# Layer 3 in tiles of two, plain last LSTM units, a new start and norms on ScalarE in a four-layer graph network

## The chip, the cores and the metric

The kernel runs on one core of one Trainium2 chip. The metric is the device time of one execution in microseconds (us). Before the change it is 2455.06 us, the median of three runs (2454.82, 2455.06, 2457.53). A core has five engines[...]: TensorE (PE; its weight loads are the row PEld) for matrix products, VectorE (DVE), ScalarE (ACT), GpSimd (POOL) and SyncE (SP), which here only starts transfers (DMAs). ScalarE can start transfers too. Products land in PSUM, everything else lies in SBUF.

## The reference

The input x has 128 graphs of 64 nodes with 256 features, and one 64x64 adjacency matrix `adj`. Four layers follow, each with a residual sum and a layer norm:

```python
x = _layernorm(x + L0(x, adj))   # A_hat x, two linear layers, each with a batch norm over all rows
x = _layernorm(x + L1(x, adj))   # Chebyshev-like aggregation by 2L/lambda_max - I, attention, GELU MLP
x = _layernorm(x + L2(x, adj))   # two GCN layers, then LSTMs over windows of 1, 2, 3 and 4 nodes
x = _layernorm(x + L3(x, adj))   # graph attention
```

What bears on the change:

- Layer 0: `deg = sum of A+I over rows + sum over columns - diagonal`, `dinv = deg**-0.5`, `A_hat = (A+I) * dinv * dinv`.
- Layer 1 needs the largest eigenvalue of the adjacency matrix.
- Layer 2: for p = 1 to 4 the nodes are cut into windows of p; an LSTM runs over the p nodes of a window and its last state replaces the last node of the window. Each p works on what the one before left.
- Layer 3: `Wh = h W`, `e[i,j] = s1[i] + s2[j]` with `s1 = Wh a1`, `s2 = Wh a2`; a leaky ReLU (slope 0.2), minus infinity where `adj` is 0, softmax over j, `h' = attention @ Wh`.

All arithmetic is float32.

## The kernel before, in words

**Tiling.** The 128 graphs are 16 blocks of 8. A block is four tiles of 128 rows (two graphs each) by 256 features: 128x1024 numbers. `tm` sees a slot as four tiles (rows on partitions), `fm` as two chunks of features on partitions. Four blocks form a group (`hT[g]`, tiles named h77 to h80). There are four PSUM tiles of 128x1024 (`PS`) and a stock of SBUF slots of the same size (`mem`), into which buffers of earlier layers are put back when they are no longer needed, so that a slot can be called x70, h77, rows or wL.

**Order.** Work is written as Python generators, which yield steps (engine, estimated time, PSUM tiles and slots needed) ahead of the instructions. `flow` runs streams of such generators: each stream has a width (how many at once) and a priority. At each turn it takes the step that can start soonest by its estimates, so the estimates set the order of the instructions on every engine; it is fixed when the program is built. Changing an estimate or a stream's width reorders instructions far away.

**Start (lines 236 to 427).** The adjacency matrix goes twice, block-diagonally, into `bdA` and its transpose into `bdAT`, all four on SP, and into `adj2` (two on ScalarE, for the masks `cap1` and `cap3`). Block 0 of x and W1 follow on ScalarE's queue; W2 and six small columns go on SP ahead of the other blocks of x. VectorE adds the identity, takes three sums and combines them (L410 to L421), POOL takes the power -1/2 (L422), and a TensorE product (L426) and a VectorE scaling (L427) give `AhT`, which the first aggregation (helper L324) needs.

**Layer 0.** `first_block` aggregates a block (L324), multiplies by W1 (L348) and takes statistics; `eig` finds the eigenvalue by 26 squarings meanwhile. After the first batch norm `second_block` multiplies by W2 (L554); after the second, `end_block` applies it (ScalarE, L625), transposes (L342), adds x (VectorE, L633) and ends with `ln_steps`.

**Layer norms.** `stats` (L275 to L277) takes mean and variance per tile on VectorE, POOL takes the power -1/2 of four numbers a row, about 1.03 us. Then `ln_steps` lets VectorE subtract and multiply, four instructions (L288); `ln_steps_act` lets VectorE make the product -mean*rstd (L313) and ScalarE do scale and bias, four instructions (L316). Before the change `ln_steps` ends layers 0 and 1, `ln_steps_act` serves layer 3.

**Layer 2.** A unit (`unit`, `lstm`) is an LSTM over all windows of one p in a group. Its first step is plain (L932). For the further steps the kernel uses a form of Strassen's multiplication on two halves of the windows: seven products instead of eight, in stages (`stage1` to `stage4`, helper L1000), with copies and sums on VectorE (L1059, L1066, L1068), copies on ScalarE (L1038, L1040) and differences on VectorE and POOL between them. `units_of` makes two units of p = 4 for the last group, of 16 windows times 16 graphs, so that their halves have 128 columns.

**Layer 3 (`last_block`).** One block at a time: load x (L1273), bring the state back to rows (ScalarE L1278, TensorE L342), add, norm, transpose (L336), multiply by W with two more columns for s1 and s2 (L1308), 16 small score products of 64x64 (L1327, L1330), leaky ReLU and softmax on ScalarE and VectorE (L1337 to L1350), division by the sum on POOL (L1352), transposition (L1358, L1360), aggregation (L1366), residual (L1370), norm, store (L1374). Two blocks of the first three groups may run at once, at the lowest priority, four of the last group, at a high one. Two LSTM units may run at once.

Of the kernel before, what the change touches and what calls it, by code (L numbers as in the profile page):

```python
# [15 lines left out]
P = 128  # L16
# [16 lines left out]
def kernel(ctx: ExitStack, tc: tile.TileContext, a: dict, out: bass.AP):  # L33
# [206 lines left out]
    for s in range(2):  # L240
        h = halves[s]
        nc.sync.dma_start(bdA[h, h], a["adj"])
        nc.sync.dma_start(bdAT[h, h], a["adjT"])
        nc.scalar.dma_start(adj2[h, :], a["adj"])
        for m in (bdA, bdAT):
            G.memset(m[h, halves[1 - s]], 0.0)
# [9 lines left out]

    cap1 = ctile([P, N], "cap1")
    V.tensor_scalar(cap1, adj2, 0.0, BIG, ALU.is_gt, ALU.mult)
    V.tensor_scalar(cap1, cap1, -1.0e9, None, ALU.add)

    cap3 = ctile([P, N], "cap3")
    V.tensor_scalar(cap3, adj2, 0.0, 2.0, ALU.not_equal, ALU.mult)
    V.tensor_scalar(cap3, cap3, -1.0, BIG, ALU.add, ALU.mult)

# [4 lines left out]
    def stats(y, n=NT):  # L269

        st = sm.tile([P, n, 6], F32, tag="ln_st", name="ln_st")
# [33 lines left out]
    def ln_steps_act(y):  # L305

        yield step("V", 2.7)
        mv, rs = stats(y)
        yield step("G", 1.0)
        G.tensor_tensor(rs, rs, neghalf[:, :NT], ALU.pow)  # L310
        yield step("V", 0.2)
        nm = sm.tile([P, NT], F32, tag="ln_nm", name="ln_nm")
        V.scalar_tensor_tensor(nm, mv[:, :, 0], -1.0, rs, ALU.mult, ALU.mult)  # L313
        yield step("S", 2.4)
        for t in range(NT):
# [16 lines left out]
    def to_fm(ps, y):  # L332

        for c in range(2):
            for t in range(NT):
                T.transpose(ps[:, c, t * P : (t + 1) * P], y[:, t, c * P : (c + 1) * P], ident)  # L336

    def to_tm(ps, yT):

        for t in range(NT):  # L340
# [48 lines left out]
    with c0:  # L389
        ep = c0.enter_context(tc.tile_pool(name="eig", bufs=2))  # L390

        first = mem.take()
        nc.scalar.dma_start(tm(mem[first]), x_blk[0])
        W1T = load_w(wp, "W1T", a["L0_gnn_W1"], queue=nc.scalar)
        W2T = load_w(wp, "W2T", a["L0_gnn_W2"])
        cols = {k: load_col(wp, f"l0{k}", a[f"L0_gnn_{k}"]) for k in ("b1", "g1", "be1", "b2", "g2", "be2")}
# [11 lines left out]

        An = ctile([P, P], "An", wp)
        V.tensor_tensor(An, bdA, ident, ALU.add)  # L410
        tmp = etile("etmp")
        V.tensor_tensor(tmp, bdAT, ident, ALU.add)
        d3 = etile("d3", 3, 1)
        V.reduce_sum(d3[:, 0:1], An, axis=AX.X)
        V.reduce_sum(d3[:, 1:2], tmp, axis=AX.X)
        tmp = etile("etmp")
        V.tensor_tensor(tmp, An, ident, ALU.mult)
        V.reduce_sum(d3[:, 2:3], tmp, axis=AX.X)
        dinv = etile("dinv", 1, 1)
        V.tensor_tensor(dinv, d3[:, 0:1], d3[:, 1:2], ALU.add)  # L420
        V.tensor_tensor(dinv, dinv, d3[:, 2:3], ALU.subtract)  # L421
# [10 lines left out]
        def eig():  # L432
            Sy = etile("Sy", bufs=1)
            yield step("V", 1.2)
            V.tensor_tensor(Sy, bdA, bdAT, ALU.add)
# [75 lines left out]
        def first_block(i):  # L511
            if i:
# [3 lines left out]
            else:  # L516
                xs = first
# [53 lines left out]
        tasks = [(None, lambda: first_block(0), 1), (None, eig, 0)]  # L571
        tasks += [(None, lambda i=i: first_block(i), 2) for i in blocks if i]
# [45 lines left out]
    def end_block(i):  # L618
# [17 lines left out]
        yield from ln_steps(x)  # L636
        mark("end", i)

    def block(i):
# [196 lines left out]
        yield from ln_steps(x)  # L836
# [13 lines left out]
    av = load_w(gw, "av", a["L3_gnn_a"])  # L850
    bl = load_col(gw, "bih", a["L2_gnn_bih"])
# [50 lines left out]
    def lstm(p, n, parts, x_of, out_of):  # L902
# [79 lines left out]
        mem.give(s_o)  # L982

# [138 lines left out]

    def gcn_block(i):
# [61 lines left out]
    def unit(p, g, w0, nw, b0, nb):  # L1185
# [4 lines left out]
        parts = [(slice(q * hn, (q + 1) * hn), nw // 2 if even else nw) for q in range(2)]  # L1190

        def half(ap, q):

            if even:
# [74 lines left out]
    def last_block(i):  # L1269
        yield step("Q", 4.0, sl=1)  # L1270
        s_x = mem.take()
        x = tm(mem[s_x])
        nc.sync.dma_start(x, XD[i])  # L1273
        yield step("S", 2.2, sl=1)
        s_h = mem.take()
        hb = fm(mem[s_h])
        for c in range(2):
            S.copy(hb[:, c, :].rearrange("p (b n) -> p b n", b=8), hT_block(i)[:, c, :, :].rearrange("p n b -> p b n"))  # L1278
        yield step("T", 1.0, ps=1)
        ps = PS.take()  # L1280
        to_tm(tm(PS[ps]), hb)
        mem.give(s_h)
        mark("read", i)
        yield step("V", 1.3, ps=-1)
# [245 lines left out]
```

## Time and profile before

| | us or share |
|---|---|
| the profiled execution | 2454.4 |
| its span, first to last instruction | 2452.6 |
| TensorE busy | 2353.9 (96%) |
| VectorE / ScalarE / POOL busy | 1274.4 / 1095.9 / 572.8 |
| mean granted TensorE clock | 0.982 |
| last LSTM products run | 2376.2 to 2376.9 |
| last store issued at | 2448.73 |

The busy time of TensorE includes stretches at a lower clock, in which the same product takes longer. Share of busy time is an average over stages with different limits, so the tables by stretches of time say more: each line gives a stretch, its length, the busy time of each engine in it (with the number of instructions), the granted clock, the busy share of the DMA engines and the GB/s moved. In the answers on single instructions the first number is the start, the second the duration, both in us, and brackets hold the idle time before and what ended it. A product of float32 with 128 or 256 columns stands as two records in the trace, a transposition as one.

### The profile page before, as it was taken

How to read it: one execution, taken by the hardware profiler on the slowest of the kernel's cores; microseconds unless marked ns; L12 is line 12 of the kernel's file. 1: busy time of each engine (PE TensorE's matmuls, PEld its weight loads, DVE VectorE, ACT ScalarE, POOL GpSimd, SP SyncE). 2: the span in 40 equal slices, each digit the busy share in tenths (PEclk: the TensorE clock that was granted, in tenths of full speed). 3: DMA queues.
4: the chain of work that ended last, by engine and by line, in shares of the span. 5: the costliest groups of instructions: out<-in, count | busy, mean ns of one | idle time of the engine just before them, and what ended most of it. 6: DMA issues, size and time to landing. Idle time of an engine off the chain costs nothing. (4 is left out here: it accounts for less than half of the span.)

```text
span 2452.6 us, 35349 instructions
## 1 busy us (share of the span) xinstructions
PE 2353.9 (96%) x14468; PEld 1818.8 (74%) x14468; DVE 1274.4 (52%) x2965; ACT 1095.9 (45%) x1916; POOL 572.8 (23%) x416
## 2 busy tenths in 40 slices
PE   8999888999999999999999999999999999999986
PEld 5544466767667767675766888899999889888874
DVE  4542387657455645484552433345344455455664
ACT  2256332333444343434434444445435465556774
POOL 0000034233323222343132222222222221222211
PEclk9999899999999999999999999999999999999997
DMA  5110110100000000000100000000000010000111
GB/s 171 43 52 0 40 36 27 44 3 15 1 9 10 18 9 10 1 9 35 44 26 11 16 1 1 1 18 1 1 1 18 1 35 10 26 18 18 61 53 44
DMA packets 40499, 57.60 MB, mean 23 GB/s; under 512 B 4624, under 2 KB 33936, under 8 KB 40336
## 3 DMA queue, kind: packets, MB, share of 16 engines
q1 hardware_dynamic: 39376, 54.25, 6.8%
q8 instruction: 113, 1.85, 0.3%
q10 hardware_dynamic: 960, 1.08, 0.1%
q14 instruction: 50, 0.41, 0.1%
HBM read 38.55 MB, written 16.78 MB: 23 GB/s over the span
## 5 line engine op out<-in xcount | busy, mean ns | idle before, releaser
L1000 PE MATMUL ps<-x,x 128*128 128x256 f32 (+1 forms) x1024 | 228.4, 360 | 0.0
L1000 PEld LDWEIGHTS ps<-x,x 128*128 128x128 f32 x1024 | 179.8, 190 | 19.5 <-DVE t L1046 0.4
L1000 PE MATMUL ps<-t,x 128*128 128x256 f32 (+1 forms) x800 | 178.5, 359 | 1.4 <-ACT x L1040 1.4
L1000 PEld LDWEIGHTS ps<-t,x 128*128 128x128 f32 x800 | 140.5, 190 | 18.9 <-ACT x L1040 2.0
L932 PE MATMUL ps<-h,wL 128*128 128x144 f32 (+2 forms) x552 | 131.8, 393 | 0.0
L348 PE MATMUL ps<-t,W1T 128*128 128x512 f32 x256 | 116.0, 597 | 0.0
L932 PEld LDWEIGHTS ps<-h,wL 128*128 128x128 f32 x552 | 87.9, 190 | 37.7 <-issue 36.8
L285 POOL TENSOR_TENSOR ln_rs<-ln_rs,neghalf 128x4 f32<-128x4 f32 x48 | 49.6, 1033 | 202.1 <-DVE ln_rs L277 202.0
L944 ACT ACTIVATE t<-ps,bih 128x512 f32<-128x512 f32 (+3 forms) x116 | 68.5, 642 | 57.7 <-PE ps L932 57.6
L275 DVE BATCH_NORM_STATS2 ln_st<-x 128x6 f32<-128x256 f32 x240 | 92.0, 403 | 0.7
L1059 DVE COPY x<-ps 128x256 f32<-128x256 f32 (+3 forms) x84 | 30.7, 366 | 118.6 <-PE ps L1000 118.5
L297 POOL TENSOR_TENSOR ln_rs<-ln_rs,neghalf 128x4 f32<-128x4 f32 x32 | 36.6, 1145 | 230.9 <-DVE ln_rs L277 230.8
L1076 ACT ACTIVATE x<-x,bih 128x512 f32<-128x512 f32 (+3 forms) x84 | 53.1, 632 | 77.9 <-DVE x L1066 77.7
L932 PE MATMUL ps<-h,x 128*128 128x256 f32 x384 | 87.1, 379 | 0.8 <-ACT t L1152 0.8
L1000 PE MATMUL ps<-h,x 128*128 128x256 f32 (+1 forms) x416 | 84.4, 333 | 1.1 <-DVE x L1059 0.6
L932 PEld LDWEIGHTS ps<-h,x 128*128 128x128 f32 x384 | 72.7, 190 | 10.9 <-ACT t L1152 1.2
L348 PEld LDWEIGHTS ps<-t,W1T 128*128 128x128 f32 x256 | 46.2, 191 | 45.9 <-issue 45.9
L288 DVE TENSOR_SCALAR x<-x,ln_mv,ln_rs 128x256 f32<-128x256 f32 x144 | 63.3, 495 | 31.5 <-POOL ln_rs L285 31.5
L1066 DVE TENSOR_TENSOR x<-ps,x 128x512 f32<-128x512 f32 (+3 forms) x84 | 48.5, 579 | 57.4 <-PE ps L1000 46.1
L1076 ACT ACTIVATE t<-t,bih 128x512 f32<-128x512 f32 (+3 forms) x59 | 36.9, 629 | 86.1 <-DVE t L1066 85.9
L944 ACT ACTIVATE x<-ps,bih 128x512 f32<-128x512 f32 (+3 forms) x88 | 51.6, 639 | 50.2 <-PE ps L932 50.1
L276 DVE BATCH_NORM_AGGREGATE ln_mv<-ln_st 128x2 f32<-128x6 f32 x448 | 71.5, 166 | 0.0
(663 smaller groups left out, 5691.6 us busy)
## 6 DMA issues: line engine op xcount, KB each, us to landing
t<-in_x_dram SPq DMA_DIRECT2D x25, 512.0 KB, 4.0
xd<-x SPq DMA_DIRECT2D x16, 512.0 KB, 2.6
x<-xd SPq DMA_DIRECT2D x8, 512.0 KB, 3.3
out_dram<-x SPq DMA_DIRECT2D x8, 512.0 KB, 2.9
h<-in_x_dram SPq DMA_DIRECT2D x6, 512.0 KB, 4.1
t<-xd SPq DMA_DIRECT2D x6, 512.0 KB, 3.3
out_dram<-t SPq DMA_DIRECT2D x6, 512.0 KB, 2.9
wL<-in_L_gnn_Wih_dram SPq DMA_DIRECT2D x2, 1024.0 KB, 5.0
```

What stands on the lines that cost most here:

```text
L275: V.bn_stats(st[:, t, :], y[:, t, :])
L276: V.bn_aggr(mv[:, t, :], st[:, t, :])
L285: G.tensor_tensor(rs, rs, neghalf[:, :NT], ALU.pow)
L288: V.tensor_scalar(y[:, t, :], y[:, t, :], mv[:, t, 0:1], rs[:, t : t + 1], ALU.subtract, ALU.mult)
L297: G.tensor_tensor(rs, rs, neghalf[:, :NT], ALU.pow)
L348: T.matmul(ps[:, c, :], w[:, k, (off + c) * P : (off + c + 1) * P], yT[:, k, :], start=(k == 0), stop=(k == nk - 1),)
L932: T.matmul(spread(fm(PS[ps])[:, j, :n], q), WL[p][0][:, k, m], x_of(0, q)[:, k], start=(k == 0), stop=(k == 1),)
L944: S.activation(of(sl)[:, j], fm(PS[ps])[:, j, :n], AF.Tanh if g == 2 else AF.Sigmoid, bias=bias(g, c))
L1000: T.matmul(dst, WS[p][name](k, g), y[:, k], start=first and k == 0, stop=k == 1, skip_group_check=not first)
L1059: V.tensor_copy(y[:, 1, :], v[:, 0, :])
L1066: V.tensor_tensor(y[:, 0:2, :], v[:, 2:4, :], y[:, 0:2, :], ALU.add)
L1076: S.activation(of(act[g])[:, 0], of(act[g])[:, 0], f, bias=bias(g, 0))
```

## The change

Five parts, in the lines of the kernel after:

1. **Start.** The four adjacency loads go two on SP and two on ScalarE. `adj2` is no longer loaded but made from `bdA` later, with the masks. Three blocks of x are loaded early, on SP, ScalarE and SP, W1 after the second. W2 and five of the six columns are issued by a task, `later_loads`, behind the first blocks. The degree comes from two VectorE instructions with a running sum.
2. **Norms.** `ln_steps_act` takes any number of tiles and replaces `ln_steps` at the end of layers 0 and 1.
3. **Layer 3.** `last_block` takes a first tile and a number of tiles; the last group goes as eight half blocks of two tiles, the others as whole blocks. The scores come from two products (block-diagonal ones times s2 spread by the identity, and the identity times s1 broadcast). The mask is applied before the leaky ReLU, which is one VectorE instruction; the maximum goes in as the bias of four exponentials, which also give the sums; the division moves behind the aggregation, into the residual sum.
4. **Last two LSTM units.** The units of 16 graphs are no longer split in halves and go by `plain_steps`: per step four pairs of gates, each of eight products of 256 columns.
5. **Streams.** The last two units have a stream of their own, so three units can run at once; four whole blocks of layer 3 may run at once instead of two; the last group's buffers are not lent again.

The diff, cut to its core:

```diff
-        nc.sync.dma_start(bdAT[h, h], a["adjT"])
-        nc.scalar.dma_start(adj2[h, :], a["adj"])
+        nc.scalar.dma_start(bdAT[h, h], a["adjT"])
...
     def ln_steps_act(y):
-        yield step("V", 2.7)
+        n = y.shape[1]
+        yield step("V", 0.68 * n)
...
-        for t in range(NT):
+        for t in range(n):
             S.activation(
...
-        first = mem.take()
-        nc.scalar.dma_start(tm(mem[first]), x_blk[0])
-        W1T = load_w(wp, "W1T", a["L0_gnn_W1"], queue=nc.scalar)
-        W2T = load_w(wp, "W2T", a["L0_gnn_W2"])
-        cols = {k: load_col(wp, f"l0{k}", a[f"L0_gnn_{k}"]) for k in ("b1", "g1", "be1", "b2", "g2", "be2")}
+        early = [mem.take() for _ in range(3)]
+        for i, q in enumerate((nc.sync, nc.scalar, nc.sync)):
+            q.dma_start(tm(mem[early[i]]), x_blk[i])
+            if i == 1:
+                W1T = load_w(wp, "W1T", a["L0_gnn_W1"], queue=nc.scalar)
...
+        def later_loads():
+            for k in cols:
+                if k != "b1":
+                    yield step("Q", 1.0)
+                    nc.sync.dma_start(cols[k], a[f"L0_gnn_{k}"])
+            yield step("Q", 6.0)
+            nc.sync.dma_start(W2T, by_chunk(a["L0_gnn_W2"]))
+            yield step("V", 1.2)
+            V.tensor_tensor(adj2, bdA[:, :N], bdA[:, N:], ALU.add)
...
+        V.scalar_tensor_tensor(Sy, bdA, 1.0, bdAT, ALU.mult, ALU.add, accum_out=d3[:, 0:1])
+        V.scalar_tensor_tensor(tmp, bdA, 1.0, ident, ALU.mult, ALU.mult, accum_out=d3[:, 1:2])
+        V.scalar_tensor_tensor(dinv, d3[:, 0:1], 1.0, d3[:, 1:2], ALU.add, ALU.subtract)
...
-        yield from ln_steps(x)
+        yield from ln_steps_act(x)
         mark("end", i)
...
-        yield from ln_steps(x)
+        yield from ln_steps_act(x)
         mark("l1", i)
...
+        if len(parts) == 1 and p > 1:
+            yield from plain_steps(p, n, us, of, bias, x_of, lambda ap: spread(ap, 0), last_h, s_cell, s_h, h_at)
+            return
...
+    def plain_steps(p, n, us, of, bias, x_of, shaped, last_h, s_cell, s_h, h_at):
+        for s in range(1, p):
+            def products(pair):
+                for j, (g, c) in enumerate(pair):
+                    for k in range(2):
+                        T.matmul(shaped(dst), WL[p][0][:, k, m], x[:, k], start=(k == 0), stop=False)
+                    for k in range(2):
+                        T.matmul(dst, WL[p][1][:, k, m], of(s_h)[:, k], start=False, stop=(k == 1))
...
+                    S.activation(of(sl)[:, j], fm(PS[ps])[:, j, :n], AF.Tanh if g == 2 else AF.Sigmoid, bias=bias(g, c))
...
+            for c in range(2):
+                cell = of(s_cell)[:, c]
+                ta, sa = yield from products(((0, c), (2, c)))
+                tb, sb = yield from products(((1, c), (3, c)))
+                G.tensor_tensor(A[:, 1], A[:, 0], A[:, 1], ALU.mult)
+                V.tensor_tensor(cell, cell, F[:, 0], ALU.mult)
+                V.tensor_tensor(cell, cell, A[:, 1], ALU.add)
+                S.activation(A[:, 1], cell, AF.Tanh)
...
+        if nb < BG:
+            parts = [(slice(0, 2 * hn), nw)]
...
-    def last_block(i):
+    def last_block(i, t0=0, nt=NT):
...
-                T.matmul(
-                    pe[h, t, :], s12[h, t, 1:2].to_broadcast([N, N]), ident[h, h], start=True, stop=False
-                )
-        S.activation(low, pe, AF.Copy, scale=0.2)
-        V.tensor_tensor(e, pe, low, ALU.max)
-        V.tensor_tensor(e, e, bc_mid(cap3, NT), ALU.min)
-        V.tensor_tensor(e, e, bc_last(mx, N), ALU.subtract)
-        S.activation(e, e, AF.Exp)
-        V.reduce_sum(sums, e, axis=AX.X)
-        G.tensor_tensor(e, e, bc_last(sums, N), ALU.mult)
+        G.tensor_tensor(d, bc_mid(unit2, nt), bc_last(s12[:, :nt, 1], N), ALU.mult)
+        T.matmul(pe, bdones, d, start=True, stop=False)
+        T.matmul(pe, ident, bc_last(s12[:, :nt, 0], N), start=False, stop=True)
+        V.tensor_tensor(e, pe, bc_mid(cap3, nt), ALU.min)
+        V.scalar_tensor_tensor(e, e, 0.2, e, ALU.mult, ALU.max)
+            S.activation(e[:, t, :], e[:, t, :], AF.Exp, bias=mx[:, t : t + 1], accum_out=sums[:, t : t + 1])
...
-        V.tensor_tensor(x, tm(PS[ps]), x, ALU.add)
+        for t in range(nt):
+            V.scalar_tensor_tensor(
+                x[:, t, :], tm(PS[ps])[:, t, :], sums[:, t : t + 1], x[:, t, :], ALU.mult, ALU.add
+            )
...
+    last = [last_of(i) for i in range(early)]
+    end = [last_of(i, t, 2) for i in range(early, NBLK) for t in range(0, NT, 2)]
...
-            Stream(4, 2, last[early:]),
+            Stream(4, 2, end),
             Stream(2, 3, gcn),
             Stream(6, 4, seq),
-            Stream(2, 5, units),
-            Stream(2, 6, last[:early]),
+            Stream(2, 5, units[:-2]),
+            Stream(2, 5, units[-2:]),
+            Stream(4, 6, last),
```

## The prediction

> **What bounds the kernel now.** I read the page's shares and slices first, then busy time by stage, then TensorE's waits, then single instructions in time order.
>
> ```profile
> PE 2353.9 (96%) x14468; PEld 1818.8 (74%) x14468; DVE 1274.4 (52%) x2965; ACT 1095.9 (45%) x1916; POOL 572.8 (23%) x416
> ...
> PE   8999888999999999999999999999999999999986
> ```
>
> TensorE is busy for 2353.9 of 2452.6 us, so only 98.7 us of idling and the stretches at a reduced clock can be won; elsewhere an edit counts only by the TensorE work it adds or removes. The stages (columns: length, then busy PE, PEld, DVE, ACT, POOL, then PE clock, DMA share, GB/s):
>
> ```profile
> 0.00:10.00 10.00, 0.00 (x0) 0.00 (x0) 2.70 (x15) 0.11 (x1) 1.96 (x14) 1.00 0.59 168
> ...
> 290.00:300.00 10.00, 6.28 (x28) 5.91 (x29) 5.58 (x21) 5.58 (x8) 1.01 (x1) 0.50 0.32 97
> ...
> 310.00:320.00 10.00, 6.45 (x43) 5.73 (x42) 10.00 (x33) 7.61 (x11) 2.59 (x3) 0.93 0.30 100
> 320.00:330.00 10.00, 8.35 (x19) 4.40 (x20) 9.74 (x31) 1.07 (x2) 6.42 (x4) 0.56 0.00 0
> ```
>
> ```profile
> 2300.00:2377.00 77.00, 68.67 (x662) 59.15 (x660) 51.31 (x175) 56.78 (x119) 15.95 (x17) 1.00 0.19 63
> 2377.00:2453.00 76.00, 49.65 (x408) 35.62 (x408) 36.50 (x129) 39.95 (x71) 11.11 (x13) 0.77 0.11 36
> ```
>
> By such tables the 99 us lie so: 10.6 in the first 20 us, 4 at the first batch norm, 24.6 in 280-400 (entry into layer 1), 9.7 in 400-800, 7.8 in 800-2000, 7.7 in 2000-2300, 8.3 in 2300-2377, 26 after the last LSTM product (2376.9). From 310 to 390 VectorE is busy for 73 of 80 us: there it is the bound. The waits name the same places (us in total, times, longest):
>
> ```profile
> PE ps L426 <- DVE etmp L424: 10.2, 1, 10.2
> PE ps L1358 <- POOL wL L1352: 7.6, 1, 7.6
> PE ps L348 <- DVE t L782: 6.3, 1, 6.3
> ```
>
> The start and one knot at the entry into layer 1, in time order (start, duration):
>
> ```profile
> 7.07 0.29 DVE L435 TENSOR_TENSOR Sy<-bdA,bdAT 128x128 f32<-128x128 f32 x1 [2.69 <-DMA bdAT<-in_adjT_dram]
> ...
> 11.39 3.63 PE L324 MATMUL ps<-AhT,t 128*128 128x128 f32 x16 [0.45 <-DVE AhT L427]
> ...
> 299.69 0.16 DVE L894 COPY Wx<-ps 128x4 f32<-128x4 f32 x1 [3.12 <-PE ps L885]
> ```
>
> The chain of waits covers only the last 29 us: one full block going alone through scores, aggregation, norm and store.
>
> [...] block 0's 16 records from 11.39 run 0.22 us apart, later ones 0.11. [...] Here one small issue takes SP 0.57 us, but the fourth lands 3.9 us after its issue, behind block 0's load. [...] in the trace no load stands before such a norm.
>
> **The change part by part.**
>
> *Start.* Four adjacency issues sat on SP, the last from 2.62; VectorE began at 7.07. Now each queue issues two, ahead of every x block; ScalarE's two old ones (0.74 to 2.21) had landed by 3.85, so I put the start at 4.0. VectorE's chain to dinv took 2.05 us; the new one (two fused sums instead of three adds and three reductions, but with five cap instructions put between them) has about ten instructions, again 1.9. POOL, scaling, product and copy stay 2.3. Block 0's product can begin at 8.2, when its x (issued at 2.0, 4.5 to landing by the DMA table, three more 512 KB behind it) has come. Blocks 0, 1 and 2 now go in a row; the state "0 and 1 aggregated" comes at 8.2 + 3.5 (half clock) + 1.8 = 13.5 against 16.8: **-3.2 us**, between -4.5 and -1 (x or W1 late). It persists, since TensorE is 100% busy from 20 to 150. W2, columns and caps are needed only after 150.
>
> *Norms that end layers 0 and 1.* Each loses four VectorE subtract-multiplies (1.38 a block) for one 0.17 and four ScalarE activations (2.08). In ScalarE's new order nine layer-0 blocks do so before the first GELU (396 in before): VectorE -11 us, ScalarE +19, of the 110 us from 280 in which ScalarE was busy 43. Also the score-column product now precedes the first layer-1 aggregation instead of splitting it; the knot above (3.1 us of VectorE, a copy to ScalarE at 310.4 that could come at about 304) goes. Against it: ScalarE runs 15 affine activations (10.7 us) before the first norm, which so ends 3 us later than before; 16 more queue behind the second copy; and PSUM copies that feed products can stand behind a norm, 2.1 us each. TensorE idles 14.7 us in 310-390 and loses some 9 to low clock from 290 to 330. I take **-8**, between -14 and +4. The 16 norms ending layer 1 fall where TensorE is 97-99% busy, VectorE 57-60%, ScalarE 39%: 0, between -1 and +3.
>
> *Layer 3.* Per block, TensorE: 16 small score products took 0.93 us, two of 256 columns take four records of 0.218, 0.9. ScalarE loses the 0.37 leaky pass and a 0.42 exponential, gains four of 64 columns with running sum: no row[...]. VectorE loses a subtract and a sum (0.42 each), gains four fused 256-wide steps (0.42 like the norm's fused steps, against one of 1.22). POOL's 0.61 moves ahead of the scores. Per block these cancel within 1 us: 0.
>
> *Plain last units.* Six steps change. Old: 56 products of 128 columns, two records of 0.111, 12.4 us; new: 32 of 256, two of 0.218, 14.0: **+9.1** TensorE in all. VectorE loses 12 copies and sums (0.28 to 0.42) and two differences per step, some 28 us, ScalarE some 19 (8 gate activations of 0.47 for 20 shorter passes), just where (2300-2377) TensorE stalls on them.
>
> *Streams.* (4,2) and both last units now run together, and four early layer-3 blocks instead of two. Idle in 2000-2377 is 16 us; I take **-5**, between -12 and 0.
>
> *The end.* In TensorE's new order some 54 us of layer-3 work (at full clock) stand behind the last LSTM product, against 37: five full and four half blocks against five partly finished ones. So that product comes 17 us earlier for this alone, and the rest gets longer. The final store is not a half block: block 11, a full one whose x load is the last, takes TensorE after the second-stage products of the first half blocks. Until then ScalarE has, in order, about 40 us: eight strided half copies of 0.6, block 11's 1.09, some 17 norms of 0.52 before the half blocks' own 16, PSUM copies of 0.25 to 1.0, exponentials, a table load of 1.28. VectorE then has 8 us before block 11's add. From there one block alone: add 1.2, stats 2.4, POOL 1.0, norms with another block's exponentials between 3.3, transposes and copy 2.4, products 3.6, scores 1.5, softmax 2.4, transpose and copy 1.0, aggregation 2.5, scaling 1.7, stats and norm 5.5, store 3.9 (2448.73 to the end in before), 20 handovers of 0.06, cold clock 2: 36-40. So 88 us against 75.7: **+12**. Bounds: 76, if four more chains in flight only fill gaps; 106, if ScalarE's 56 us there stretch as its 40 did.
>
> **Sum.** Last LSTM product: 2376.9 - 3.2 - 8 + 9.1 - 17 - 5 = 2352.8; plus 88: 2440.8, 11.8 below the span. The profiled execution took 2454.4, 1.8 over its span; the runs' median is 0.7 above it: **2443**.
>
> **Rivals.** Differences under 0.2% (4.9 us) can't be told from none.
> (a) The two engines' relief is hidden: TensorE's idling in 310-390 stays, since the norm's longer path (one instruction more, behind ScalarE's queue) takes the place of VectorE's. For: 15 affine passes stand before the first norm. Against: VectorE 10.00 and 9.74 in the two slices shown. Step 2 becomes 0: 2451.
> (b) Slower, by one mechanism: the deferred full block at the end. With a tail of 106, 2461; it turns slower than before from a tail of 105 (75.7 + 24.1 won earlier + 4.9). For: before spread its tail over 1.9 times ScalarE's work. Against: the other chains lacked partners, not an engine.
> (c) More concurrency fills all gaps (tail 76, layer 1 -12): 2427.
>
> **Chances.** Forecast 0.50 (own range 2433-2450), (c) 0.17, (a) 0.15, (b) 0.18. (a) lies at the 0.2% bound and is taken as no change. Faster 0.67, same 0.15, slower 0.18. To leave out no more than 2 in 10: 2428 to 2462.
>
> **What would show it.** Right: first aggregation near 8.2; VectorE below 9 tenths from 310 to 390; an LSTM end near 2353; the last store from a full block. Wrong: adjacency landing after 5; ScalarE, not VectorE, ahead of TensorE's waits at 290-330; TensorE idle between the last units' steps; a tail beyond 105.

## The result, and where the time went

The changed kernel takes 2480.06 us (median of four runs, 2478.72 to 2480.56) against 2456.11 us (2454.82 to 2457.53) before on the same chip: a ratio of 1.0099, with a 95% interval of 1.0084 to 1.0113. It is 24 us slower, where 2443 us were forecast. The profiled span is 2478.3 us against 2452.6.

The page of the kernel after, shares and TensorE's slices:

```profile
PE 2369.7 (96%) x13700; PEld 1812.0 (73%) x13700; DVE 1219.0 (49%) x2868; ACT 1159.2 (47%) x2091; POOL 570.8 (23%) x426
...
PE   8999889999999999998989999999999999999996
```

VectorE has 55 us less to do and ScalarE 63 us more, as the edits say, and still TensorE is busy 15.8 us longer and idle 9.9 us longer (108.6 against 98.7). The busy time holds part of the loss too: by the trace's clock records 69.0 us of it run at half clock, 53.9 before. The products of 512 columns of L342 begin 0.854 us apart there and 0.429 us apart at full clock (medians), so of the 15.8 an estimated 7.5 are clock. The slices hardly show where: two 8s in the middle that were 9s. The stages do (columns: length, then busy PE, PEld, DVE, ACT, POOL, then PE clock, DMA share, GB/s):

```profile
0.00:10.00 10.00, 3.13 (x13) 2.84 (x14) 2.61 (x16) 0.00 (x0) 1.94 (x14) 1.00 0.69 220
290.00:300.00 10.00, 9.58 (x44) 9.21 (x45) 6.33 (x24) 6.00 (x11) 2.02 (x2) 0.50 0.31 91
...
310.00:320.00 10.00, 4.85 (x27) 4.28 (x26) 10.00 (x36) 8.20 (x13) 3.54 (x3) 0.82 0.22 74
320.00:330.00 10.00, 9.33 (x24) 4.28 (x23) 9.20 (x30) 4.11 (x6) 6.43 (x5) 0.67 0.00 0
...
400.00:1320.00 920.00, 882.53 (x5850) 611.38 (x5850) 501.69 (x1108) 394.19 (x507) 272.44 (x165) 0.99 0.05 17
...
2385.00:2478.30 93.30, 66.95 (x425) 47.33 (x423) 52.22 (x218) 56.39 (x140) 17.65 (x24) 0.83 0.12 40
```

The start looks as forecast, the entry into layer 1 in sum a little better than before (TensorE idles 20.8 us in 280 to 400, 24.6 before). The line of 400 to 1320 is the one that matters: 37.5 us without TensorE work, where the kernel before had 15.4:

```profile
400.00:1320.00 920.00, 904.62 (x5977) 630.03 (x5976) 521.14 (x1195) 364.01 (x437) 278.20 (x170) 1.00 0.05 17
```

Of the change's five parts only norms run there: the 16 that end layer 1, and the last of those that end layer 0 (up to about 540). The Strassen products of the LSTMs begin 28.5 us later than before (1341.1 against 1312.6), from there to the last LSTM product (2385.1 against 2376.9) 20 us are won back, and the end takes 93.2 us against 75.7.

TensorE's waits (us in total, times, longest) no longer name one cause:

```profile
PE ps L318 <- ACT x L1221: 9.5, 3, 5.8
PE ps L436 <- DVE etmp L434: 6.4, 1, 6.4
PE ps L342 <- DVE x L642: 5.9, 1, 5.9
...
PE ps L1419 <- POOL h L1415: 4.8, 2, 3.8
```

The second is the start (10.2 before), the last belongs to the end. The first, a graph convolution's second aggregation waiting for its ReLU, lies in 1125 to 1320 and was 0.5 to 1.0 us long before.

### The profile page after: what moved, and what is told of

Read it like the earlier page. It is cut to its first block, busy times and chain, and to the rows that moved or that the text cites. A ratio compares the mean times of both kernels' runs of the same rounds, so it can differ in the third digit from the quotient of the medians.

```text
span 2478.3 us, 33908 instructions
## 1 busy us (share of the span) xinstructions
PE 2369.7 (96%) x13700; PEld 1812.0 (73%) x13700; DVE 1219.0 (49%) x2868; ACT 1159.2 (47%) x2091; POOL 570.8 (23%) x426
## 5 line engine op out<-in xcount | busy, mean ns | idle before, releaser
L1020 PE MATMUL ps<-x,x 128*128 128x256 f32 x896 | 221.7, 380 | 0.0
L310 ACT ACTIVATE x<-x,ln_nm,ln_rs 128x256 f32<-128x256 f32 x180 | 95.6, 593 | 108.5 <-DVE ln_nm L307 108.3
L1020 PE MATMUL ps<-t,x 128*128 128x256 f32 x576 | 141.8, 380 | 2.0 <-ACT t L1060 1.8
L1020 PEld LDWEIGHTS ps<-t,x 128*128 128x128 f32 x576 | 107.8, 190 | 17.5 <-ACT t L1060 2.0
L304 POOL TENSOR_TENSOR ln_rs<-ln_rs,neghalf 128x4 f32<-128x4 f32 (+1 forms) x72 | 68.3, 949 | 222.8 <-DVE ln_rs L270 203.0
L342 PE MATMUL ps<-t,W1T 128*128 128x512 f32 x256 | 115.7, 597 | 0.7 <-ACT h L545 0.7
L948 PE MATMUL ps<-h,wL 128*128 128x192 f32 (+2 forms) x480 | 100.5, 364 | 1.0 <-ACT t L960 0.5
L948 PE MATMUL ps<-h,x 128*128 128x256 f32 x384 | 87.2, 380 | 0.8 <-ACT t L1228 0.8
L948 PE MATMUL ps<-t,wL 128*128 128x512 f32 x192 | 83.9, 593 | 0.8 <-ACT x L689 0.8
L342 PEld LDWEIGHTS ps<-t,W1T 128*128 128x128 f32 x256 | 46.3, 190 | 47.6 <-issue 46.9
L1096 ACT ACTIVATE t<-t,bih 128x512 f32<-128x512 f32 (+2 forms) x57 | 37.2, 653 | 88.7 <-DVE t L1086 88.6
L290 POOL TENSOR_TENSOR ln_rs<-ln_rs,neghalf 128x4 f32<-128x4 f32 x32 | 36.8, 1151 | 178.7 <-DVE ln_rs L270 178.6
L342 PE MATMUL ps<-t,wA 128*128 128x512 f32 x144 | 70.4, 636 | 7.4 <-ACT t L677 5.8
L1020 PE MATMUL ps<-h,x 128*128 128x256 f32 x288 | 72.5, 380 | 0.0
L1079 DVE COPY t<-ps 128x256 f32<-128x256 f32 (+2 forms) x57 | 21.6, 380 | 101.1 <-PE ps L1020 100.9
```

What stands on the lines that cost most here:

```text
L304: G.tensor_tensor(rs, rs, neghalf[:, :n], ALU.pow)
L310: S.activation(y[:, t, :], y[:, t, :], AF.Identity, scale=rs[:, t : t + 1], bias=nm[:, t : t + 1])
L342: T.matmul(ps[:, c, :], w[:, k, (off + c) * P : (off + c + 1) * P], yT[:, k, :], start=(k == 0), stop=(k == nk - 1),)
L948: T.matmul(spread(fm(PS[ps])[:, j, :n], q), WL[p][0][:, k, m], x_of(0, q)[:, k], start=(k == 0), stop=(k == 1),)
L1020: T.matmul(dst, WS[p][name](k, g), y[:, k], start=first and k == 0, stop=k == 1, skip_group_check=not first)
L1096: S.activation(of(act[g])[:, 0], of(act[g])[:, 0], f, bias=bias(g, 0))
```

## The experiments

Eighteen kernels were run beside the kernel before, whose medians lay between 2455.1 and 2456.0 us. "Last product" is the end of the last LSTM product in the profile, "end" what follows it, "idle" is TensorE's idle time in 400 to 1320, all in us.

| kernel | median | ratio to before | last product | end | idle |
|---|---|---|---|---|---|
| before | 2455.5 | 1 | 2376.9 | 75.7 | 15.4 |
| changed | 2480.1 | 1.0099 | 2385.1 | 93.2 | 37.5 |
| e1 norms ending layer 1 back | 2452.4 | 0.9987 | 2359.4 | 92.0 | 17.6 |
| e2 norms ending layer 0 back | 2448.1 | 0.9968 | 2349.7 | 93.6 | 15.1 |
| e3 both back | 2451.3 | 0.9983 | 2354.8 | 93.9 | 14.9 |
| e4 before, layer 1's norms moved | 2458.9 | 1.0018 | 2382.5 | 75.9 | 18.6 |
| e5 old order, on ScalarE | 2448.9 | 0.9973 | 2353.6 | 93.5 | 15.8 |
| e6 new order, on VectorE | 2471.7 | 1.0070 | 2376.4 | 93.6 | 36.1 |
| e7 estimate 0.52 | 2463.5 | 1.0034 | 2360.4 | 100.9 | 19.9 |
| e8 estimate 0.65 | 2454.5 | 0.9995 | 2363.3 | 89.6 | 22.5 |
| e9 new order, light VectorE | 2440.7 | 0.9940 | 2346.1 | 94.0 | 12.0 |
| e10 old order, light VectorE | 2434.5 | 0.9913 | 2339.5 | 93.7 | 4.5 |
| e11 e3 with Strassen units | 2439.5 | 0.9935 | 2375.3 | 63.5 | 14.9 |
| e12 e3 with old streams | 2476.1 | 1.0082 | 2361.0 | 114.4 | 14.9 |
| e13 e11 with whole blocks | 2442.7 | 0.9945 | 2359.3 | 80.4 | 15.0 |
| e14 e5 with Strassen units | 2440.2 | 0.9935 | 2376.4 | 63.5 | 15.4 |
| e15 e2 with Strassen units | 2436.4 | 0.9921 | 2370.6 | 63.4 | 15.2 |
| e16 changed with Strassen units | 2472.4 | 1.0066 | 2405.2 | 64.1 | 37.5 |
| e17 e11 with old streams | 2469.4 | 1.0058 | 2379.0 | 87.5 | 14.8 |
| e18 e15, other margin | 2475.9 | 1.0084 | 2391.5 | 82.6 | 24.1 |

The forecast took differences under 0.2% (4.9 us) as none. Nothing is built here on a smaller step between two of these kernels either; "under the bound" means that.

### Which norms: e1 to e4

The first theory was that the norms which end layer 1 lengthen each block's path once ScalarE does them; the rivals were the norms which end layer 0, and the planner's order as such. Each undo is one line of the changed kernel (e1 the second, e2 the first, e3 both); e4 makes the second edit alone in the kernel before.

```diff
         mem.give(xin)
-        yield from ln_steps_act(x)
+        yield from ln_steps(x)
         mark("end", i)
...
         mem.give(s_y)
-        yield from ln_steps_act(x)
+        yield from ln_steps(x)
         mark("l1", i)
```

> The changed kernel with the 16 norms that end layer 1 put back on VectorE, all else as changed. In the traces the first Strassen product of the LSTMs comes at 1312.4 us before and at 1340.9 after, so 28.5 us are lost ahead of it and only about -3 in the rest. Theory N1 (the norms that end layer 1, on ScalarE, lengthen each block's path and the gaps of 400 to 1305): this kernel has its first Strassen product near 1313 and takes about 2452. Theory N0 (the norms that end layer 0 do it): it stays at 2475 to 2480. Theory O (no one edit's engine does it, the planner's new order by itself is worse): neither; any time from 2450 to 2480, and the pair of single edits does not add up.

> The changed kernel with the 16 norms that end layer 0 put back on VectorE, all else as changed. N1: first Strassen product stays near 1340 or later (the entry into layer 1 loses the 4 us it gained), time 2478 to 2486. N0: first Strassen product near 1315, time about 2454. O: anything from 2450 to 2485.

> The changed kernel with both sets of norms back on VectorE. N1 and N0 both: first Strassen product near 1310 (1312.4 less the gain at the start), time about 2450 to 2456, that is what start, layer 3, plain units and streams are worth together (forecast in sum -4). O: not nearer to 1310 than either single one by more than 5 us.

> The kernel before with only the norms that end layer 1 moved to ScalarE. N1: first Strassen product later by 20 to 30 us, time 2475 to 2485. N0: no more than 3 us from before, 2453 to 2459. O: a shift of any size, not that of the changed kernel against its counterpart without these norms.

Measured: 2452.4, 2448.1, 2451.3 and 2458.9 (for e4 a ratio of 1.0018, 1.0011 to 1.0025). Either undo alone takes back the whole loss and both together no more; one set on ScalarE costs +1.1 (e1 against e3) or -3.2 (e2 against e3), both under the bound, the two sets +28.7. N1 fell with e2 and e4, N0 with e1: no single set is the cause. Either the two sets together overload something, or the order is to blame. The first Strassen product turned out to be a poor mark, since some orders begin a unit early (1290.9 in e1, 1273.8 in e4); the last LSTM product is used from here.

### Order or engine: e5 to e8

A step is announced to the planner with an engine and a time, and the instructions that follow may go anywhere. So the two can be taken apart: e5 announces both sets as before and executes them on ScalarE; e6 announces them as the change does and executes them on VectorE. e7 and e8 move no instruction to another engine and change one estimate.

```diff
+    def ln_steps_x(y):
+        yield step("V", 2.7)
+        mv, rs = stats(y)
+        yield step("G", 1.0)
+        G.tensor_tensor(rs, rs, neghalf[:, :NT], ALU.pow)
+        yield step("V", 1.9)
+        nm = sm.tile([P, NT], F32, tag="ln_nm", name="ln_nm")
+        V.scalar_tensor_tensor(nm, mv[:, :, 0], -1.0, rs, ALU.mult, ALU.mult)
+        for t in range(NT):
+            S.activation(y[:, t, :], y[:, t, :], AF.Identity, scale=rs[:, t : t + 1], bias=nm[:, t : t + 1])
```

```diff
-        yield step("S", 0.6 * n)
+        yield step("S", 0.52 * n)
```

> The changed kernel with both sets of norms executed on ScalarE, but announced to the planner as before (VectorE 2.7, GpSimd 1.0, VectorE 1.9 us), so that TensorE's order is that of the kernel with both norms back (2451.3 us) but for a few products that stand some places elsewhere. Theory E (the engine: ScalarE carries both norms, comes late and lets TensorE wait): about 2470 to 2480. Theory O (the order that the planner makes from the new estimates is worse; the engine matters little): 2448 to 2458, first Strassen product within 5 us of that kernel's.

> The mirror: both sets of norms executed on VectorE (and without the one small product that only the ScalarE form needs), but announced to the planner as ScalarE work as in the changed kernel, so that TensorE's order is that of the changed kernel. Theory E: 2450 to 2458, TensorE's idling in 400 to 1320 back to 15 to 20 us. Theory O: 2470 to 2485, idling there 30 us or more as in the changed kernel (37.5).

> The changed kernel with one number changed: the ScalarE step of the norm is estimated at 0.52 us a tile (what an activation of it takes by the trace of before) instead of 0.6. No instruction is added, removed or moved to another engine; only the planner's order can change. Theory E: within 5 us of the changed kernel, 2475 to 2485. Theory O: another order, so another time, most likely between 2445 and 2465, as the three orders already seen.

> The same with 0.65 us a tile. Theory E: 2475 to 2485. Theory O: another order; with e7 it shows how wide the spread over orders is: at least one of the two lies over 10 us below the changed kernel.

Measured: 2448.9, 2471.7, 2463.5, 2454.5. Busy time in 400 to 1320 of e5 (first fence) and e6 (second):

```profile
400.00:1320.00 920.00, 904.25 (x5972) 631.01 (x5970) 489.36 (x1110) 406.94 (x524) 276.89 (x170) 0.99 0.05 17
```

```profile
400.00:1320.00 920.00, 883.86 (x5853) 614.75 (x5852) 532.23 (x1162) 351.39 (x418) 273.09 (x164) 0.98 0.05 17
```

e5 carries all norms on ScalarE (406.94 us, more than the changed kernel's 394.19) and TensorE is busy for 904.25 us; e6 carries them on VectorE and TensorE has only 883.86. In the traces TensorE's work stands in e6 in the same order as in the changed kernel (1732 groups of products, one by one), and in e5 as in e3 but for one group. So the greater part of the loss goes with the order, not with the engine. Of the changed kernel's 28.7 us against e3, the order by itself makes 20 (e6 against e3); with ScalarE in that order 8 more are lost, and with ScalarE in the old order 2.5 won, which is under the bound. e7 and e8, the same instructions on the same engines, take 16.6 and 25.5 us less than the changed kernel (the estimate is that of layer 3's norms too, so that the end is reordered as well).

### What is wrong with that order: e9 and e10

The longest gap of 1100 to 1320 in the changed kernel, in time order (start, duration; PE, DVE and ACT only):

```profile
1129.90 0.45 DVE L293 SCALAR_TENSOR_TENSOR x<-x,ln_mv,rows 128x256 f32<-128x256 f32 x1
...
1132.18 3.72 PE L354 MATMUL ps<-Wg,x 128*128 128x256 f32 x16
...
1133.96 1.22 DVE L669 SCALAR_TENSOR_TENSOR x<-x,x 128x1024 f32<-128x1024 f32 x1
1135.10 1.22 DVE L841 TENSOR_TENSOR t<-ps,t 128x1024 f32<-128x1024 f32 x1
...
1140.17 1.28 DVE L296 SCALAR_TENSOR_TENSOR x<-t,ln_rs,x 128x256 f32<-128x256 f32 x3 [0.90 <-POOL ln_rs L290]
...
1143.68 1.19 DVE L1218 TENSOR_TENSOR x<-ps,rb 128x1024 f32<-128x1024 f32 x1
...
1144.90 1.06 ACT L1221 ACTIVATE x<-x 128x1024 f32<-128x1024 f32 x1 [11.55 <-DVE x L1218]
...
1146.01 3.58 PE L318 MATMUL ps<-bdAT,x 128*128 128x128 f32 x16 [5.79 <-ACT x L1221]
```

The convolution's product (L354) ends at 1135.9. The bias add that takes it out of PSUM (L1218) comes at 1143.68: since 1119 VectorE has worked through three affine norms (L293, L296) of other blocks in a row, and a sum (L841), the last of these norms and the statistics of a norm that ends layer 1 stand in its queue between the product's end and the add. ScalarE, idle for 11.55 us, applies the ReLU at once, and TensorE, with nothing else planned in front of the aggregation, has stood for 5.79 us. VectorE, busy 49% of the span, is the bound for these 20 us. The add's input was ready 7.8 us before it began. VectorE even stands idle for 0.90 us before 1140.17, waiting for POOL, and still the add comes behind the passes that follow there.

VectorE's queue is not the only one that comes late. Of the 20 gaps over 0.3 us in 400 to 1320 (37 us in all) the two longest, 5.95 us before 537.36 and these 5.79, stand behind VectorE's queue (the kernel before has one of 5.20 us before 535.22). Others, of 2.08 us before 652.51 and of 2.33 us before 1226.90, stand behind ScalarE's. For the latter the input of a copy (L764) is ready at 1220.9, and a norm's four activations (L310) and other work go ahead of it:

```profile
1222.21 1.09 ACT L310 ACTIVATE x<-x,ln_nm,ln_rs 128x256 f32<-128x256 f32 x2 [4.30 <-DVE ln_nm L307]
...
1225.85 1.00 ACT L764 COPY t<-ps 128x1024 f32<-128x1024 f32 x1
...
1226.90 2.88 PE L774 MATMUL ps<-t,t 64*64 64x64 f32 x61 [2.33 <-ACT t L764]
```

e9 and e10 leave out the second pass of the affine norms, in the new order and in the old one:

```diff
             dst = y if len(b.shape) == 2 else b
-            V.scalar_tensor_tensor(dst[:, t, :], y[:, t, :], rs[:, t : t + 1], o, ALU.mult, ALU.add)
```

> The changed kernel without the second pass of the affine norms of layer 1 (the four VectorE instructions of L296 for each norm; this work is left out), every estimate kept, so TensorE's order is the changed kernel's but for a few products. In the trace of the changed kernel the longest gap of 1100 to 1310 (5.79 us, at 1146.01) waits for a VectorE add that comes 7.8 us after its product, behind three such norms in a row. Theory Q (the new order bunches blocks so that VectorE's queue, busy 22 of 25 us there, comes late): idling of TensorE in 400 to 1320 falls from 37.5 to under 22, time falls by 18 to 30, to 2450 to 2462. Theory D (the new order puts dependent products too close together, and the latencies of the chain alone make the gaps): idling stays above 30, time above 2468.

> The control: the same work left out of the kernel with both norms back on VectorE (2451.3). Q: its order hardly waits for VectorE in 400 to 1320 (15 us of idling, one wait of 5.2 for VectorE), so it gains 3 to 9 us, to 2442 to 2448; what the two orders differ by falls from 28.7 to under 14. D: the difference stays above 22.

Measured 2440.7 and 2434.5: the new order gains 39.4 us, the old one 16.8, and what divides them falls from 28.7 to 6.2. e9 in 400 to 1320:

```profile
400.00:1320.00 920.00, 908.01 (x5991) 633.96 (x5990) 436.17 (x1000) 410.09 (x530) 279.16 (x171) 0.99 0.05 17
```

TensorE's idling is 12.0 us instead of 37.5, with ScalarE as full as ever. The idling and the difference between the orders are as theory Q gave them; both times lie below its ranges (2450 to 2462 and 2442 to 2448), so the lighter norms save more than it reckoned. The new order is one in which VectorE comes late. Two reservations: the edit also shortens each block's path by four instructions, so that it does not divide queue from path everywhere; for the longest gap the lines above do. And e6, with 30 us more VectorE work in 400 to 1320 than the changed kernel and TensorE's work in the same order, is 8 us faster, so that VectorE's load alone does not make the loss.

### The last units, the streams, the end: e11, e12, e16, e17, e13

On e3, whose first 1320 us are like those of before, the other parts were undone. Strassen units again (e11; e16 the same in the changed kernel), old streams (e12; e17 both), whole blocks in the last group (e13, on e11):

```diff
-        if nb < BG:
-            parts = [(slice(0, 2 * hn), nw)]
```

```diff
-            Stream(2, 5, units[:-2]),
-            Stream(2, 5, units[-2:]),
-            Stream(4, 6, last),
+            Stream(2, 5, units),
+            Stream(2, 6, last),
```

```diff
-    end = [last_of(i, t, 2) for i in range(early, NBLK) for t in range(0, NT, 2)]
+    end = [last_of(i) for i in range(early, NBLK)]
```

> The kernel with both norms back (2451.3), its last two LSTM units by Strassen's form in halves of 128 columns again; streams and layer 3 as changed. Forecast of the prediction's step: plain units cost 9.1 us of TensorE and take stalls away. If the relief is worth more (theory R): this is slower, 2454 to 2464, last LSTM product not earlier than 2353. If the 9.1 us are simply paid (theory W): faster, 2442 to 2448, last LSTM product near 2346.

> The kernel with both norms back, with one stream for all LSTM units (two at once) and two early layer-3 blocks at once, as before; plain units and half blocks kept. Forecast of the prediction's step: the new streams are worth 5 us (0 to 12), so 2451 to 2463 here, TensorE's idling in 2000 to 2300 above 5.6 and the last LSTM product later than 2354. Rival: the wider streams let layer-3 blocks run into the end and lengthen the tail (93.9 from the last LSTM product to the end against 75.7 before): then here a shorter tail, under 85, and 2440 to 2448.

> The changed kernel with nothing undone but the plain units. If the parts add up (the order ahead of 1341 us and the last units are independent): 2480.1 - 11.8 = 2468.3 (2465 to 2471), first Strassen product at 1341 as in the changed kernel, last LSTM product and tail as with Strassen units (tail near 63). If the tail depends on the order ahead: tail above 70, 2472 or more.

> Both norms back, Strassen units and the old streams (one stream for all LSTM units, two early layer-3 blocks at once): only the start and layer 3 (arithmetic, half blocks) are left of the change. If the new streams are worth their 25 us whatever the units are (theory V): 2460 to 2468, so start and layer 3 together would have cost 5 to 12. If the 25 belong to plain units, which need a third unit beside them to hide their longer steps (theory P): 2446 to 2453, near what the start's 2.7 takes off the 2455.5 of before.

> The kernel of the last but one run (both norms back, Strassen units: 2439.5 us, 63.5 us from the last LSTM product to the end), with the last group's four blocks whole instead of eight half blocks. If the half blocks shorten the end by having more chains in flight (theory H): slower, 2443 to 2452, tail above 67. If they only add instructions (theory I): faster, 2432 to 2438.

Strassen units: 2439.5 (0.9935, 0.9918 to 0.9951), 11.8 us less than e3 and below the 2442 to 2448 of theory W. TensorE's busy time is 2349.3 against 2358.9 us, but most of these 9.6 us are clock, not work: after 2000 e3 is busy for 17.5 us at half clock and e11 for 2.8, by the same two spacings an estimated 7 us. Counted from the start of one product to the next (a longer pause as 0.3 us), the Strassen products take 755.2 us in e11, and in e3 674.5 and the plain ones 83.2: the plain form costs 2.5 us. TensorE's idling from 2000 to the end is the same, 33.9 in both. Theory W's way is not found either: the last LSTM product comes 21 us later (2375.3, not 2346) and the end is 30 us shorter. The end of e3, then that of e11:

```profile
2354.80:2448.60 93.80, 66.97 (x424) 47.31 (x422) 52.17 (x218) 56.27 (x140) 17.64 (x24) 0.83 0.12 40
...
2375.30:2438.80 63.50, 43.95 (x317) 31.04 (x314) 40.87 (x182) 45.88 (x117) 15.39 (x22) 0.91 0.20 67
```

Behind the last product 44 us of TensorE work are left instead of 67, at a clock of 0.91 instead of 0.83: eleven stores are still to come against nine, but their blocks are further on. The planner orders the end anew with the units, and the 11.8 us belong to the form and that order together. In the changed kernel itself the same undo gives 2472.4 (e16; 7.7 less, below the 11.8 and just outside of what addition gave), with its order's 37.5 us of idling in 400 to 1320 untouched.

Streams: with the old ones 2476.1 under plain units and 2469.4 under Strassen units, so the new streams are worth 24.8 and 29.9 us with either form. e12 lies above its forecast (2451 to 2463), and its rival fails too: the end is longer, 114.4 us against 93.9. With the old streams TensorE idles longer after 2000: 52.8 us against 33.9 (e12 against e3), 45.5 against 33.9 (e17 against e11). The third LSTM unit and the four early blocks were not tried apart. Theory P falls; e17 lies 1.4 us above theory V's range. Start plus layer 3 without the streams (e17; the last group's buffers are still not lent again) make the kernel before 13.9 us slower (1.0058, 1.0043 to 1.0073). The end of e17, stores on SP and then TensorE's products:

```profile
2434.52 0.37 SPq L1457 DMA_DIRECT2D out_dram<-t  x1
2462.72 0.37 SPq L1457 DMA_DIRECT2D out_dram<-wA  x1
```

```profile
2424.79 1.08 PE L1446 MATMUL ps<-x,t 64*64 64x256 f32 x8
2435.65 2.80 PE L330 MATMUL ps<-ident,wA 128*128 128x128 f32 x8 [9.78 <-ACT wA L310]
```

All blocks but one are stored by 2434.5; the last goes alone for another 28 us, and TensorE waits 9.78 us for its norm. A possible reason is that only two early blocks go at a time while the half blocks, of higher priority, pass them; the new arithmetic may cost too. This is not shown: the two were not tried apart. Whole blocks for the last group: 2442.7 against 2439.5 (e13), 3.2 us, which is under the bound and just short of theory H's range, so that the worth of the half blocks stays open.

### Versions that beat both: e14, e15, e18

> Strassen units together with both sets of norms on ScalarE in the old order. On ScalarE alone the old order gave 2448.85 against 2451.3, so if that holds and adds up: 2437 (2435 to 2438.5). If it was noise of the order of a few us: 2438.5 to 2442.

> Strassen units, norms ending layer 1 on ScalarE (announced as such), norms ending layer 0 on VectorE. Additive: 2448.1 - 11.8 = 2436.3 (2433 to 2440). If the gain of 11.8 belongs to one order only: outside of that.

> The fastest so far (2436.4: Strassen units, norms ending layer 0 on VectorE, the rest as changed), with the planner's margin for VectorE steps raised from 0.5 to 1.5 us, so that it plans them behind others sooner. If a planner that allows VectorE to be late makes better orders (theory M): 2426 to 2434, TensorE's idling in 400 to 1320 below 15. If it is one more order without a system (theory O): 2436 to 2460.

e14 took 2440.2, no less than e11: the 2.5 us of e5 did not add up. e15 (Strassen units, norms ending layer 0 on VectorE, everything else as changed) took 2436.4, as the sum said, a ratio of 0.9921 to before (0.9906 to 0.9936): it beats both kernels. e18 raised the planner's margin for VectorE in e15:

```diff
-MARGIN = {"T": 2.0, "V": 0.5, "S": 0.5}
+MARGIN = {"T": 2.0, "V": 1.5, "S": 0.5}
```

It took 2475.9, 39.5 us more and outside of what either theory gave. To know that VectorE comes late is not enough to plan it away with this one number.

### The change as a staircase

| | median | step |
|---|---|---|
| before | 2455.5 | |
| + start and layer 3 (e17) | 2469.4 | +13.9 |
| + streams (e11) | 2439.5 | -29.9 |
| + plain last units (e3) | 2451.3 | +11.8 |
| + norms ending layer 0 (e1) | 2452.4 | +1.1 |
| + norms ending layer 1 (changed) | 2480.1 | +27.6 |

The last two steps depend on their order: taken the other way round they are -3.2 (e2) and +32.0. Each step also holds the order that the planner made anew for it; only for the norms was that taken apart.

## Why the prediction was wrong

**The step that failed** is the part on the norms, which put the two sets at -8 and 0; together they cost 28.7 us (the changed kernel against e3). Its last sentence shows how: "The 16 norms ending layer 1 fall where TensorE is 97-99% busy, VectorE 57-60%, ScalarE 39%: 0, between -1 and +3." It priced the engines, with shares taken over 400 us, and took the order as given. As long as the order stays, the engine matters as little as that sentence says (on VectorE or on ScalarE, in the old order: 2451.3 and 2448.9). But a norm announced on another engine is a new input to the planner for 32 norms, and the order that it made with both sets left TensorE 22.6 us more without work in 400 to 1320 than e3's. With the half clock behind the gaps (17.8 us of busy time there against 7.7), 30 us lie between e3's last LSTM product and the changed kernel's. No rival named this; (b), the one on the slower side, put the loss at the end, where 93.2 us stayed well under its point of 105. What the new order does wrong is shown for some of its gaps; why the planner takes this one when both sets are announced on ScalarE, and a better one when either is, is not settled.

**Start.** Right up to 158 us. The start of the changed kernel in time order:

```profile
3.91 0.29 DVE L425 SCALAR_TENSOR_TENSOR Sy<-bdA,bdAT 128x128 f32<-128x128 f32 x1 [3.91 <-DMA bdAT<-in_adjT_dram]
...
7.67 1.65 PE L318 MATMUL ps<-AhT,t 128*128 128x128 f32 x6 [0.44 <-DVE AhT L437]
```

3.91 for a forecast 4.0, 7.67 for 8.2 (before, the fourth load landed 4.3 us after its issue at 2.62, not 3.9); the last product with W1 begins 2.6 us earlier (155.6 against 158.2) for -3.2. "It persists" failed. At the entry into layer 1, before and then after:

```profile
285.53 0.29 DVE L487 TENSOR_TENSOR LnT<-etmp,ident 128x128 f32<-128x128 f32 x1
...
286.20 0.28 DVE L870 COPY rb<-ps 128x128 f32<-128x128 f32 x1
...
286.62 2.31 PE L342 MATMUL ps<-ident,h 128*128 128x128 f32 x8 [4.39 <-DVE rb L870]
```

```profile
282.46 9.27 ACT L634 ACTIVATE h<-h,bn2sh,bn2sc 128x512 f32<-128x512 f32 x13 [3.29 <-DVE bn2sh L511]
...
285.40 0.29 DVE L495 TENSOR_TENSOR LnT<-etmp,ident 128x128 f32<-128x128 f32 x1
...
286.20 0.28 DVE L886 COPY rb<-ps 128x128 f32<-128x128 f32 x1
...
286.63 1.94 PE L336 MATMUL ps<-ident,h 128*128 128x128 f32 x8 [2.37 <-DVE rb L886]
```

The last product with W2 ends 2.4 us earlier and ScalarE begins the batch norm 3.1 us earlier, but one squaring more of the eigenvalue is left over, VectorE finishes `LnT` at 285.7 for 285.8 before, and the two copies behind it free the way for TensorE at 286.6, to 0.01 us the same. The gain was bounded by a second chain that had been just hidden.

**Norms ending layer 0.** VectorE lost 12.1 us in 310 to 390 (61.27 busy against 73.37; forecast 11), and TensorE's idling there went from 14.7 to 13.3. Rival (a) was right, by the longest gap in its reason too. Before, TensorE did wait for VectorE there (6.3 us before a product of L348, 4.1 before a transposition of L336); after, it waits 5.81 us for a ScalarE copy (L677) behind two of a norm's activations, which wait for the one VectorE instruction more (L307); another 5.15 us still wait for VectorE:

```profile
340.11 2.34 POOL L715 TENSOR_TENSOR t<-t,rows 128x1024 f32<-128x1024 f32 x1
340.18 2.29 DVE L307 SCALAR_TENSOR_TENSOR ln_nm<-ln_mv,ln_rs 128x4 f32<-128x4 f32 x1 [0.86 <-POOL ln_rs L304]
...
342.50 1.09 ACT L310 ACTIVATE x<-x,ln_nm,ln_rs 128x256 f32<-128x256 f32 x2 [3.91 <-DVE ln_nm L307]
...
343.50 0.99 ACT L677 COPY t<-ps 128x1024 f32<-128x1024 f32 x1
...
344.54 2.07 PE L342 MATMUL ps<-t,wA 128*128 128x512 f32 x2 [5.81 <-ACT t L677]
```

Alone these norms are worth nothing (e1 against e3), for a forecast of -8.

**Plain units.** The +9.1 was too much. It put Strassen's records 0.111 us apart; with the short pauses between its products the 672 records of the last two units come 0.120 us apart on average (755.2 less 674.5 us), and the plain form costs 2.5 us more. What the relief of VectorE and ScalarE takes away can only lie in such pauses; the idling from 2000 to the end is the same with either form, under the new streams. That the step as a whole is +11.8, near the 9.1, is luck.

**Streams and end.** The streams' -5 was far too small (-25 to -30), and the zero for layer 3 too kind (start and layer 3 together +13.9). One term that the profile of before had no row for is measured: the four exponentials with a running sum begin 0.33 us apart, so 1.3 us a block. The end was forecast at 88 us with a whole block alone at last; it is 93.2 (66.95 us of TensorE busy at a clock of 0.83), and its last store is a whole block. Leaving the norms' -8 out, the sum gave 2360.8 for the last product and 2448.8 for the span; e3, that is the change without its norms, has 2354.8 and 2448.6. Only the sum agrees, and that is luck: -3.2 for the start and 0 for layer 3 stand against +13.9, -5 for the streams against -25 to -30, and the misses cancel.

## What to carry to other kernels

Where a list planner sets the order, an edit has two prices: the engine's, which the profile gives, and the order's, which it doesn't. Take them apart by executing the new form under the old announcement, and the old form under the new one, before you reject or keep an edit: here the engine's price was too small to tell in the old order (-2.5 us) and 8 in the new, the order's 20, and one changed estimate moved the same instructions by 26. Before a gain at one place is carried to the end, look for the chain that was hidden behind it, and for what each busy engine's queue holds in front of the one instruction that TensorE needs.

## What the runs showed of the hardware that was not expected

The longer of two gaps was not the one that cost half clock. In the changed kernel a gap of 2.33 us, before 1226.90, was followed by half clock, and one of 2.84 us, before 1243.23, by none. In its trace and in that of the kernel before, the times from one change of the granted clock to the next are multiples of 3.41 us (1 to 539 of them), so the changed kernel is cut here in slices of that length between such changes (stage columns as above, clock third from the end):

```profile
1224.35:1227.76 3.41, 1.08 (x33) 0.86 (x30) 2.35 (x3) 3.41 (x5) 0.00 (x0) 1.00 0.64 197
1227.76:1231.17 3.41, 3.41 (x100) 3.41 (x99) 0.09 (x1) 1.01 (x1) 0.00 (x0) 0.50 0.67 264
...
1238.00:1241.41 3.41, 2.39 (x12) 1.75 (x10) 3.41 (x10) 0.00 (x0) 0.00 (x0) 1.00 0.00 0
1241.41:1244.83 3.42, 1.60 (x14) 1.60 (x15) 0.91 (x4) 1.06 (x1) 2.41 (x2) 1.00 0.01 2
1244.83:1248.24 3.41, 2.90 (x22) 2.15 (x21) 1.38 (x4) 1.69 (x3) 1.09 (x2) 1.00 0.00 0
```

The 2.33 us lie in one slice; the 2.84 are split into 1.02 and 1.82. Of the 1382 such slices at full clock in these two traces 22 are followed by one at half clock: TensorE idles in them for 1.55 to 3.41 us. In the 1360 others it idles for 1.82 us at most. In these traces, then, half clock goes with the idle time within one slice, and a longer gap that was split cost none.

Beside POOL some VectorE instructions took up to five times as long. In the changed kernel, 400 to 1320, the pass L296 takes 0.45 to 0.49 us in all 103 cases in which POOL is idle at its start. In the 13 others it took 0.48 twice and otherwise 1.48 to 2.56:

```profile
530.28 2.34 POOL L808 TENSOR_TENSOR h<-h,rows 128x1024 f32<-128x1024 f32 x1
530.34 2.56 DVE L296 SCALAR_TENSOR_TENSOR x<-t,ln_rs,x 128x256 f32<-128x256 f32 x1 [0.90 <-POOL ln_rs L290]
```

It ends 0.28 us after POOL's, and the gap of 5.95 us before 537.36 stands behind it. All 27 VectorE instructions of that stretch which last over 1.5 us run beside one of POOL (66.2 us of VectorE's 501.7); the same instructions without POOL beside them take at most 1.23. So a part of VectorE's busy time here is lengthening beside POOL, not work.

The exponentials that also sum stand as two instructions in the trace, 64 pairs in the changed kernel, the second of 0.19 us:

```profile
1995.58 0.35 ACT L1432 ACTIVATE x<-x,mx 128x64 f32<-128x64 f32 x1
1995.84 0.19 ACT L1432 ACTIVATION_READ_ACCUMULATOR x<-x,mx 128x1 f32 x1
1995.93 0.33 ACT L1432 ACTIVATE x<-x,mx 128x64 f32<-128x64 f32 x1
```

With overlaps a pair for 64 columns takes 0.33 us (median from start to start).
